# The q, k and v projections of a windowed attention by seven products instead of eight, with a rearranged schedule around them

## The chip, the cores and the metric

The kernel runs on one core of a Trainium2 chip. The metric is the device time of one execution in microseconds. The kernel before took 3387.21 us as the median of three runs (3384.05 to 3391.96).

The engines are named as in the profile: PE is TensorE (matmuls; PEld its weight loads), DVE is VectorE, ACT is ScalarE, POOL is GpSimd, and SP is the queue from which all transfers are issued. Each works through its own instructions in order; they wait for one another by semaphores.

## The reference

An attention layer and a feed-forward layer (FFN), each between two layer norms and with a residual. All values are float32. The batch is 4 x 2048 tokens of 512 features; the FFN has 2048 hidden features and weights of its own for every batch, mixed from eight experts.

```python
x = x + ln(attn(ln(x)))          # ln without scale or offset
x = x + ln(ffn(ln(x)))

def attn(x):                     # 16 heads of 32, windows of 128
    q, k, v = split(x @ w_qkv)
    # a window attends to itself and to the window on either side
    return softmax(q * 32**-0.5 @ k_ctx.T) @ v_ctx

def ffn(x):                      # the batch's weights come from a gate
    h = relu(x @ gate_w1.T + gate_b1)
    g = mean_over_tokens(h @ gate_w2.T + gate_b2)          # [batch, 8]
    mW1, mW2 = W1 + sum_e g[e] * TW1[e], W2 + sum_e g[e] * TW2[e]
    mb1, mb2 = b1 + g @ Tb1, b2 + g @ Tb2
    return gelu(x @ mW1.T + mb1) @ mW2.T + mb2
```

## The kernel before, in words

**Two stages.** The attention comes first, for all four batches; the FFN follows. Tokens are cut into 64 windows of 128 (`W_`) and into 16 blocks of 512 (`K`, four windows each, four blocks a batch). Between the stages, and for the gate, the normalised x lies transposed in DRAM (`xT_d`), the residual in `x1_d`.

**The attention's slots.** A loop over 256 slots (L552) handles window `i // 4` and head group `i % 4` (four heads). Nothing is scheduled by a planner: the order in the source is the order on each engine. In slot i the order is:

1. `first` hooks, then `scores(i + 1)`: four heads' scores on PE (L403) into two PSUM tiles of pool `ps_s`, and two reductions on DVE (L412) for the negative row maxima;
2. `rest` hooks (norms, residuals and their transfers), and from slot 84 on some steps of the mixer (below): 1, 1, 2 and 2 or 3 in the four slots of a window (L563);
3. `turn(i, 0)` and `turn(i, 1)`: transposes of the probabilities on PE (L440), copied from PSUM by ACT (L442);
4. the first half of the slot's `dense` piece, if it has one: four matmul records of a projection (L352) or of the gate (L163) into the single buffer of `ps_m`;
5. two exponentials of slot i + 1 on ACT (L425), `turn(i, 2)`, two more exponentials;
6. the second half of the dense piece, and the reading of its bank (`projected`: q and v by ACT, k by DVE; `gate_sum` by ACT);
7. the first `aux` hook, `values(i)` on PE (L457), the other `aux` hooks.

The hooks of a window `W_` are: in slot 4W_+4 the transposes of its output ("out transposes", L223) and their scaling by DVE with statistics (L230, L88), in 4W_+5 the residual and its store, in 4W_+6 the normalisation `normed`, and in 4W_+7 the transposes of xn2 (L252), copied by ACT and stored to `xT_d`. Each window has tiles `a`, `x1` and `xn2` of its own in two buffers each, and the residual input `xr` in three.

**Projections.** Block K > 0 is projected in the twelve slots from `s0 + 4`, with `s0 = 16K - 20`: four slots for q, four for k, four for v, each one output chunk of 128 features (for v: of 128 tokens) as four matmuls of 512 columns. A float32 matmul is two records in the trace. The four slots ahead of them transpose the block's normalised x (L338, copied by DVE, L339); most of those four have a gate's piece as `dense`. Block 0 is projected ahead of the slots. Slots 12 to 15, 240 to 247 and 252 to 255 have no dense piece.

**The gate.** 15 blocks have their gate in the attention (`gate_at`), the last has all of its gate in the FFN's block 0 (`gate_last`).

**The mixer** (L102) is a generator. A step multiplies one expert's 128 x 1024 piece into an accumulator on DVE (L144), and every ninth step forms sums of quarters (L152 to L155) and later stores them. A step first issues the load for the step three further on, from SP, into four buffers `exps`. There are 4 batches x 2 weights x 8 pieces x 9 = 576 steps; a batch's must be done before its FFN.

**The FFN** already multiplies 2 x 2 blocks by seven products (Strassen-Winograd), with sums of weights from the mixer and sums of x from `right_sums` (L272, `tT`). A block has a first half of four sets (`begin`, `middle`, `end`; matmuls at L606) and a second half of seven products (`second`, `product2`, L699), 6.9 us each. `product2` ends by asking for the weights three products later (`load_second`, L690), which need the buffer that this product reads. Beside them run mixing steps: four in a set, two in each product of the second half; in block 0 none in the sets. At the end of each batch the last block's `end` loads the next batch's first weights (L284).

Of the kernel before, what the change touches and what calls it, by code (L numbers as in the profile page):

```python
# [34 lines left out]
def sandwich(ctx: ExitStack, tc: tile.TileContext, x, w_qkv, gw1, gb1, gw2, gb2, w1, b1, w2, b2, tw1, tb1, tw2, tb2, out):  # L35
# [133 lines left out]

    def gate_end(b, hsum, spare, bank):  # L170
# [47 lines left out]
        b: const.tile([P, KC, NBLK], F32, name=f"hsum_{b}") for b in range(NB)  # L218
# [70 lines left out]
    with ExitStack() as actx:  # L289
        qkvp = actx.enter_context(tc.tile_pool(name="qkvp", bufs=2))  # L290
        work = actx.enter_context(tc.tile_pool(name="work", bufs=2))
        ps_s = actx.enter_context(tc.tile_pool(name="ps_s", bufs=2, space=PSUM))
# [68 lines left out]

        def span_of(W_):
            b, w = divmod(W_, NW)
            lo, hi = max(w - 1, 0), min(w + 1, NW - 1)
            return b * NW + lo, hi - lo + 1

        def open_window(W_):
            win[W_] = {
                "nm": small.tile([P, H], F32, tag="nm", name=f"nm_{W_}"),
                "den": small.tile([P, H], F32, tag="den", name=f"den_{W_}"),  # L370
                "pr": {},
                "prT": {},
            }
            if W_ == NWA - 1:

                win[W_]["oT"] = oT_last
                return
            win[W_] |= {
                "a": work.tile([P, D], F32, tag="a", name=f"a_{W_}"),
                "x1": work.tile([P, D], F32, tag="x1", name=f"x1_{W_}"),  # L380
                "xn2": work.tile([P, D], F32, tag="xn2", name=f"xn2_{W_}"),
                "oT": work.tile([P, KC, P], F32, tag="oT", name=f"oT_{W_}"),
                "xo": work.tile([P, KC, P], F32, tag="xo", name=f"xo_{W_}"),
                "x": load_tile(W_ // WB, W_ % WB, "xr", 3),
            }
# [82 lines left out]
        slots = range(-16, NS + 64)  # L468
        dense = {i: None for i in slots}
# [4 lines left out]
        for K in range(1, NBK):  # L474
            s0 = 4 * (4 * K - 5)
            if K > 1:
                for t in range(WB):
# [5 lines left out]
                    aux[s0 + t].append(lambda K=K, t=t: place_tile(K, t, nc.vector.tensor_copy))  # L483
            for n, i in enumerate((0, 1, 2)):
                for m in range(KC):
                    dense[s0 + 4 + 4 * n + m] = (
                        lambda pm, kcs, K=K, i=i, m=m: project(K, i, m, pm, kcs),
                        lambda pm, K=K, i=i, m=m: projected(K, i, m, pm),
                    )
# [10 lines left out]

        gate_at = {K: 4 * (4 * (K + 3) - 5) for K in range(11)} | {11: 204, 12: 220, 13: 236, 14: 248}
        for K, s0 in gate_at.items():
            first[s0 - 2].append(lambda K=K: load_gate(K))
            for oc in range(KC):
                dense[s0 + oc] = (
                    lambda pm, kcs, K=K, oc=oc: gate_matmuls(pm, gT_of[K], oc, kcs),
                    lambda pm, K=K, oc=oc: gate_sum(pm, K, oc, hsum_of[K // NBLK], spare),
                )
            if K % NBLK == NBLK - 1:
                b = K // NBLK  # L510
                for j, f in enumerate(gate_end(b, hsum_of[b], spare, spare_bank)):
                    late[s0 + KC + j].append(f)

# [5 lines left out]
        for W_ in range(NWA - 1):  # L519
# [3 lines left out]
            aux[4 * W_ + 7].append(lambda W_=W_: via_pt(xn2_transposes, xn2_store, W_, "ptx"))  # L523

        first[240].append(lambda: load_first(0, 0, 0, wp, "w2"))
        first[240].append(lambda: load_block(0))
# [11 lines left out]
        for n, (i, m) in enumerate((i, m) for i in range(3) for m in range(KC)):  # L538
# [3 lines left out]
            projected(0, i, m, pair[:, n % 2, :])  # L542
            if n in (2, 3, 4, 5):
                norm_stats(1, n - 2)
            if n in (5, 6, 7, 8):
                norm_tile(1, n - 5)
            if n in (8, 9, 10, 11):
                place_tile(1, n - 8, nc.vector.tensor_copy)
        scores(0)
        exponentials(0, range(4))  # L550

        for i in range(NS):  # L552
# [4 lines left out]
            if i + 1 < NS:  # L557
                scores(i + 1)

            for f in rest[i]:  # L560
                f()
            if i >= 84:
                for _ in range((1, 1, 2, 2 if W_ % 3 == 2 else 3)[g]):  # L563
# [3 lines left out]
            if dense[i]:  # L567
                pm = ps_m.tile([P, TB], F32, tag="pm", name=f"pm_{i}")
                dense[i][0](pm, range(KC // 2))
            if i + 1 < NS:  # L570
                exponentials(i + 1, (0, 1))
            if nk == 3:
                turn(i, 2)
            if i + 1 < NS:
                exponentials(i + 1, (2, 3))
            if dense[i]:
                dense[i][0](pm, range(KC // 2, KC))
                dense[i][1](pm)
# [7 lines left out]
    with ExitStack() as fctx:  # L586
# [8 lines left out]
        def home(c, i):  # L595
            return (wp, "w2") if c == i == 0 else (wts, f"w1_{c}_{i}")
# [206 lines left out]
        def load_gate_last():  # L803
            gT_last.append(wp.tile([P, KC, TB], F32, tag="w0", name="gT_last"))
            nc.sync.dma_start(gT_last[0], xT_d[NBK - 1])

        def gate_last(oc):
            pm = ps_x.tile([P, 2, Q], F32, tag="xz"[oc % 2], name=f"pmg_last_{oc}").rearrange("p a b -> p (a b)")
            gate_matmuls(pm, gT_last[0], oc)
            gate_sum(pm, NBK - 1, oc, hsum_of[NB - 1], spare)  # L810
# [8 lines left out]
            ("product", 0, 2): [lambda: gate_last(0), lambda: gate_last(1), lambda: gate_last(2), lambda: gate_last(3)],  # L819
# [5 lines left out]
        for c in range(0, HC, 2):  # L825
            for i in range(2):
                if c or i:
# [6 lines left out]
        def step():  # L834
            next(blend, None)

        def steps():
            for _ in range(2):
                next(blend, None)

        def nothing():
            pass

        for K in range(NBK):
# [5 lines left out]
            for c in range(0, HC, 2):  # L850
                n = K * (HC // 2) + c // 2
                S = begin(n)
                middle(n, S, before, step if K else nothing)
# [5 lines left out]
            for j, _ in enumerate(second(K, before, steps, load_x1)):  # L859
# [64 lines left out]
```

## Time and profile before

| what | us |
|---|---|
| median of three runs | 3387.21 |
| the profiled execution | 3387.08 |
| its span, first to last instruction | 3385.3 |
| start of the first FFN matmul (L606) | 1790.34 |
| L352 (projections), both forms, busy on PE | 720.5 |
| L163 (gate, without the last block), busy on PE | 223.9 |
| L440 (turns), busy on PE | 418.4 |
| L144 (mixing), busy on DVE; idle before it for transfers | 693.5; 209.2 |
| ACT prT, pr (L442, L425), busy with the accumulator reads | 1202 |

The page gives, for each engine, the time in which it was busy. PE's busy time says little, since ends of pipelined matmuls are modelled. The chain follows the work that ended last back through whatever released it, piece by piece: a stage whose chain is PE without gaps is set by PE. The timeline lists an engine's instructions with the idle time ahead of them and its releaser. The view of windows gives busy times in stretches, then the granted TensorE clock, the share of the DMA engines and their GB/s.

### The profile page before, as it was taken

Reading aid. Unit: us, or ns where it says so; the run is one execution under the profiler, and the core shown is the slowest. Engines: PE = TensorE matmul, PEld = TensorE weight load, DVE = VectorE, ACT = ScalarE, POOL = GpSimd, SP = SyncE. Lnnn points to the kernel's source line nnn. Section 1 sums busy time; section 2 is a strip of 40 time slices with the busy share of each in tenths; the row PEclk is TensorE's granted clock in tenths of the full one; section 3 lists DMA queues with packets and bytes.
Section 4 is the critical chain, followed back from the end, with each engine's and each line's share of the span. In section 5 each row is a group of like instructions: output and inputs, shape, how many; then the busy total and the mean of one; then the engine's idle time right before and its main releaser. Section 6 shows DMA issues by size and latency. Waiting matters only on the chain.

```text
span 3385.3 us, 55842 instructions
## 1 busy us (share of the span) xinstructions
PE 3333.6 (98%) x21712; PEld 2401.5 (71%) x21712; DVE 2043.7 (60%) x2872; ACT 1484.7 (44%) x3878; POOL 658.0 (19%) x776
## 2 busy tenths in 40 slices
PE   8999999999999999999989999999999999999998
PEld 3555655565555655566558788888888888888887
DVE  2545455688888787887784666677766663222222
ACT  2666666666666666666673111122211122222111
POOL 0100011111111111111002132233223232212222
PEclk9999999999999999999999999999999999999999
DMA  2111111466665666656676788988899883533332
GB/s 82 46 49 42 51 57 51 135 198 203 214 215 184 208 205 197 214 186 203 194 244 228 282 300 292 367 292 299 300 336 356 309 297 140 181 107 112 125 121 78
DMA packets 315194, 651.79 MB, mean 193 GB/s; under 512 B 22953, under 2 KB 88617, under 8 KB 294450
## 3 DMA queue, kind: packets, MB, share of 16 engines
q1 hardware_dynamic: 314930, 648.22, 55.4%
q8 instruction: 171, 2.80, 0.3%
q14 instruction: 93, 0.76, 0.1%
HBM read 538.03 MB, written 110.10 MB: 191 GB/s over the span
## 4 chain that ended last, share of the span: by engine, by line
PE 95%; DMA 2%; DVE 1%; ACT 1%; issue 1%; SPq 0%; DVEq 0%; ACTq 0%
PE pm L352 20%; PE px L606 12%; PE ptp L440 10%; PE px L699 10%; PE pz L699 7%; PE sc L403 7%; PE pm L163 6%; PE pz L606 6%; PE po L457 6%; PE py L699 3%; PE py2b L699 3%; PE py L606 3%; DMA exps<-in_tw 1%; PE ptx L252 1%; PE pto L223 1%; PE pt_a L338 1%
## 5 line engine op out<-in xcount | busy, mean ns | idle before, releaser
L144 DVE SCALAR_TENSOR_TENSOR acc<-exps,g,acc 128x1024 f32<-128x1024 f32 x512 | 693.5, 1355 | 214.2 <-DMA exps<-in_tw 209.2
L442 ACT COPY prT<-ptp 128x512 f32<-128x512 f32 x736 | 407.2, 588 | 525.2 <-PE ptp L440 524.6
L412 DVE TENSOR_REDUCE nm<-sc 128x2 f32<-128x768 f32 (+1 forms) x512 | 448.1, 917 | 257.6 <-PE sc L403 256.7
L425 ACT ACTIVATE pr<-sc,nm 128x384 f32<-128x384 f32 (+1 forms) x1024 | 577.2, 578 | 5.0 <-DVE nm L412 5.0
L440 PEld LDWEIGHTS ptp<-ident,pr 128*128 128x128 f32 x2944 | 332.4, 142 | 223.0 <-issue 204.5
L352 PE MATMUL pm<-xnT,wqkv 128*128 128x512 f32 x1024 | 480.1, 596 | 3.6 <-DVE k L358 1.6
L440 PE MATMUL ptp<-ident,pr 128*128 128x128 f32 x2944 | 418.4, 279 | 5.0 <-ACT prT L442 3.2
L639 ACT COPY cpa<-px 128x512 f32<-128x512 f32 x64 | 37.2, 582 | 793.6 <-PE px L606 793.6
L606 PE MATMUL px<-tT,w 128*128 128x256 f32 x1536 | 358.7, 382 | 10.5 <-DVE cpv L664 10.5
L606 PEld LDWEIGHTS px<-tT,w 128*128 128x128 f32 x1536 | 292.8, 191 | 52.9 <-DVE cpv L664 13.0
L352 PEld LDWEIGHTS pm<-xnT,wqkv 128*128 128x128 f32 x1024 | 177.5, 191 | 144.0 <-issue 136.7
L403 PE MATMUL sc<-k,q 32*128 32x384 f32 (+2 forms) x2816 | 246.2, 422 | 2.9 <-ACT pr L425 2.9
L352 PE MATMUL pm<-wqkv,xnT 128*128 128x512 f32 x512 | 240.4, 593 | 0.5 <-ACT v L360 0.5
L92 POOL TENSOR_SCALAR ve_b<-mv_b 128x1 f32<-128x1 f32 x64 | 14.2, 221 | 1136.8 <-DVE mv_b L90 1084.9
L699 PE MATMUL px<-w2s,u 128*128 128x256 f32 x1024 | 229.5, 380 | 0.7 <-ACT last L257 0.7
L457 PE MATMUL po<-prT,v 128*32 128x128 f32 x5888 | 217.6, 278 | 7.9 <-ACT prT L442 7.7
L457 PEld LDWEIGHTS po<-prT,v 128*32 128x32 f32 x5888 | 144.6, 109 | 112.0 <-issue 93.6
L163 PE MATMUL pm<-gT,gw_sb 128*128 128x512 f32 x480 | 223.9, 593 | 0.0
L425 ACT ACTIVATION_READ_ACCUMULATOR pr<-sc,nm 128x1 f32 x1024 | 217.6, 212 | 0.0
L699 PEld LDWEIGHTS px<-w2s,u 128*128 128x128 f32 x1024 | 195.1, 191 | 27.6 <-ACT last L257 0.9
L676 POOL TENSOR_TENSOR t<-u 128x512 f32<-128x512 f32 x64 | 87.5, 1367 | 465.4 <-ACT u L618 459.3
L403 PEld LDWEIGHTS sc<-k,q 32*128 32x128 f32 x2816 | 119.8, 183 | 58.1 <-issue 28.7
(127 smaller groups left out, 4423.1 us busy)
## 6 DMA issues: line engine op xcount, KB each, us to landing
exps<-in_tw SPq DMA_DIRECT2D x512, 512.0 KB, 5.4
w2s<-m2d SPq DMA_DIRECT2D x112, 1024.0 KB, 5.6
acc<-in_w SPq DMA_DIRECT2D x64, 512.0 KB, 6.0
x<-in_x SPq DMA_DIRECT2D x64, 256.0 KB, 3.1
m1d<-acc SPq DMA_DIRECT2D x64, 256.0 KB, 6.5
m2d<-acc SPq DMA_DIRECT2D x64, 256.0 KB, 6.1
w<-m1d SPq DMA_DIRECT2D x16, 1024.0 KB, 8.5
fxT<-xTd SPq DMA_DIRECT2D x16, 1024.0 KB, 7.4
```

The costliest lines, as they stand in the source:

```text
L144: nc.vector.scalar_tensor_tensor(acc, ets.pop(n), g_all[b][:, e : e + 1], acc, ALU.mult, ALU.add)
L163: nc.tensor.matmul(pm, lhsT=gw1_sb[:, kc, ts(oc, P)], rhs=xT[:, kc, :], start=(kc == 0), stop=(kc == KC - 1))
L352: nc.tensor.matmul(pm, lhsT=l, rhs=r, start=(kc == 0), stop=(kc == KC - 1))
L403: nc.tensor.matmul(scs[r // 2][:, r % 2, col : col + nj * W], lhsT=q[rows, g, ts(W_ % WB, W)], rhs=k_of[kb][rows, g, j0 * W : (j0 + nj) * ...
L412: nc.vector.tensor_reduce(st["nm"][:, h : h + 2], scs[u][:, :, : nk * W], AX.X, ALU.max, negate=True)
L425: nc.scalar.activation(pr[:, : nk * W], scs[r // 2][:, r % 2, : nk * W], AF.Exp, bias=st["nm"][:, h : h + 1], accum_out=st["den"][:, h : h ...
L440: nc.tensor.transpose(pt[:, r, :], st["pr"][g * 4 + r][:, ts(j, W)], ident)
L442: nc.scalar.copy(prT, pt)
L457: nc.tensor.matmul(st["po"][r * E : (r + 1) * E, g, :], lhsT=v_of[kb][:, jj, h * E : (h + 1) * E], rhs=prT[:, r, :], start=(j == 0), stop= ...
L606: nc.tensor.matmul(bank[:, f, :], lhsT=factor[:, f, kc * P : (kc + 1) * P], rhs=right[:, kc, :], start=(start and f == 0 and kc == 0), sto ...
L676: nc.gpsimd.tensor_tensor(t1s[c], b12, S["u"][:, :, :Q], ALU.subtract)
L699: nc.tensor.matmul(bank[:, t, :], lhsT=right(c - c % 2)[:, c % 2, ts(t, P)], rhs=w[:, c, :], start=(start and c == t == 0), stop=True, ski ...
```

## The change

Each of q, k and v of the blocks 1 to 15 is computed by seven products of half-size factors. The operands are cut into quarters of 256 x 256 (features by features for the weights, features by tokens for x); four sums of quarters of either operand are formed by DVE, those of the weights once (`left_factors`, after block 0 has used the weights, one of them in place), those of x for each block (`right_factors`, two operations in each of slots s0+4 and s0+5). A product is four matmuls of 256 columns. Some products add to the bank that an earlier one left in PSUM; ACT copies out four of the seven states of the bank and DVE adds the other three to what has been copied.

A projection still has four slots. In the slot of product 0 it stands alone, in the place of the old dense piece. In the other three an odd product (1, 3, 5) goes between the scores and the turns ("fore"), and the next even one into the old place.

Around it:

- the placing copies of x go from DVE to ACT;
- `a`, `x1` and `xn2` share one tile in two buffers, `xr` has two buffers;
- the xn2 transposes of most windows go one slot later, into the slot of a product 0;
- mixing steps in the attention follow a table of 20 in 16 slots;
- half of the last block's gate goes to slots 254 and 255; the FFN keeps the other half;
- the second tile of the FFN's first weights is loaded early, in slot 240;
- in the FFN the mixing steps are 4 in a set (2 in the last block of a batch that another follows, and in the last two sets of block 0; none in its first two), and 3, 3, 3, 3, 3, 2, 1 in the second half.

```diff
+        def left_factors(i):
+            w = wqkv[i]
+            l11, l12, l21, l22 = (w[:, 2 * j : 2 * j + 2, h * Q : (h + 1) * Q] for h in range(2) for j in range(2))
+            pool, tag = (wp2, f"s{i}") if i else (wp, "w3")
+            s = pool.tile([P, 3, 2, Q], F32, tag=tag, name=f"wsum_{i}")
+            nc.vector.tensor_tensor(s[:, 0], l21, l22, ALU.add)
+            nc.vector.tensor_tensor(l21, l11, l21, ALU.subtract)
+            nc.vector.tensor_tensor(s[:, 1], s[:, 0], l11, ALU.subtract)
+            nc.vector.tensor_tensor(s[:, 2], l12, s[:, 1], ALU.subtract)
...
+        def right_factors(K, part):
...
+            if part == 0:
+                t = work.tile([P, 3, 2, Q], F32, tag="tx", bufs=1, name=f"tx_{K}")
...
+                nc.vector.tensor_tensor(t[:, 0], r12, r11, ALU.subtract)
+                nc.vector.tensor_tensor(t[:, 1], r22, t[:, 0], ALU.subtract)
+            else:
+                t = rights[K]
+                nc.vector.tensor_tensor(r12, r22, r12, ALU.subtract)
+                nc.vector.tensor_tensor(t["T4"], r21, t["T2"], ALU.subtract)
...
+        products = (
+            ("12", "21", True, (0, 0), False),
+            ("11", "11", True, (0, 0), True),
+            ("S2", "T2", False, (0, 1), False),
+            ("S3", "T3", False, (1, 1), False),
+            ("22", "T4", False, (1, 0), False),
+            ("S1", "T1", True, (1, 1), True),
+            ("S4", "22", False, (0, 1), True),
+        )
+        def product(K, i, u, half):
+            l, r, begins, _, _ = products[u]
+            if begins and half == 0:
+                bank[0] = ps_m.tile([P, 2, Q], F32, tag="pm", name=f"pm_{K}_{i}_{u}")
...
+            for kc in range(2):
+                a, b = (left, right) if i < 2 else (right, left)
+                nc.tensor.matmul(
+                    bank[0][:, half, :],
+                    lhsT=a[:, kc, ts(half, P)],
+                    rhs=b[:, kc, :],
+                    start=(begins and half == kc == 0),
...
+        def produced(K, i, u):
...
+            if added and i == 0:
+                nc.vector.scalar_tensor_tensor(to, bank[0], QSCALE, to, ALU.mult, ALU.add)
+            elif added:
+                nc.vector.tensor_tensor(to, bank[0], to, ALU.add)
+            elif i == 0:
+                nc.scalar.mul(to, bank[0], QSCALE)
+            else:
+                nc.scalar.copy(to, bank[0])
...
-                "a": work.tile([P, D], F32, tag="a", name=f"a_{W_}"),
-                "x1": work.tile([P, D], F32, tag="x1", name=f"x1_{W_}"),
-                "xn2": work.tile([P, D], F32, tag="xn2", name=f"xn2_{W_}"),
+                **dict.fromkeys(("a", "x1", "xn2"), work.tile([P, D], F32, tag="x1", name=f"x1_{W_}")),
...
-                    aux[s0 + t].append(lambda K=K, t=t: place_tile(K, t, nc.vector.tensor_copy))
...
+                    aux[s0 + t].append(lambda K=K, t=t: place_tile(K, t, nc.scalar.copy))
+            if K > 1:
+                for part in range(2):
+                    rest[s0 + 4 + part].append(lambda K=K, part=part: right_factors(K, part))
+            for i in range(3):
+                for u in range(7):
+                    (fore if u % 2 else dense)[s0 + 4 + 4 * i + (u + 1) // 2] = (
...
+        rest[252].append(load_gate_half)
+        for n, i in enumerate((254, 255)):
+            ocs = (2 * n, 2 * n + 1)
+            dense[i] = (
...
-            aux[4 * W_ + 7].append(lambda W_=W_: via_pt(xn2_transposes, xn2_store, W_, "ptx"))
+            i = 4 * W_ + 8 if W_ < 58 and W_ % WB != 1 else 4 * W_ + 7
+            aux[i].append(lambda W_=W_: via_pt(xn2_transposes, xn2_store, W_, "ptx"))
...
+            if m == KC - 1:
+                left_factors(i)
...
+        for part in range(2):
+            right_factors(1, part)
...
+        MIXED = (0, 0, 1, 2, 1, 1, 2, 2, 1, 1, 1, 2, 1, 1, 2, 2)
...
+            if fore[i]:
+                fore[i][0](0)
+                fore[i][0](1)
+                if more:
+                    exponentials(i + 1, (0, 1))
+                fore[i][1]()
...
-                for _ in range((1, 1, 2, 2 if W_ % 3 == 2 else 3)[g]):
+                for _ in range(MIXED[i % 16]):
...
-                pm = ps_m.tile([P, TB], F32, tag="pm", name=f"pm_{i}")
-                dense[i][0](pm, range(KC // 2))
-            if i + 1 < NS:
-                exponentials(i + 1, (0, 1))
+                dense[i][0](0)
+            if more:
+                exponentials(i + 1, (2,) if fore[i] else (0, 1))
...
+                if n < 2:
+                    step = mixing(0, 0, 0, 0)
+                elif K == 0 or (k == NBLK - 1 and b + 1 < NB):
+                    step = mixing(0, 1, 0, 1)
+                else:
+                    step = mixing(1, 1, 1, 1)
...
-            for j, _ in enumerate(second(K, before, steps, load_x1)):
+            for j, _ in enumerate(second(K, before, mixing(3, 3, 3, 3, 3, 2, 1), load_x1)):
```

## The prediction

> **What bounds the kernel now.** I read the page first (engine shares and the chain that ended last), then the chain in order of time inside the attention, then the timeline of VectorE (DVE) around a window's first slot, then the busy time by stretches in the feed-forward stage (FFN).
>
> ```profile
> span 3385.3 us, 55842 instructions
> PE 3333.6 (98%) x21712; PEld 2401.5 (71%) x21712; DVE 2043.7 (60%) x2872; ACT 1484.7 (44%) x3878; POOL 658.0 (19%) x776
> PE 95%; DMA 2%; DVE 1%; ACT 1%; issue 1%; SPq 0%; DVEq 0%; ACTq 0%
> ```
>
> TensorE (PE) carries 95% of the chain. One attention slot of the chain shows what is in it:
>
> ```profile
> 1077.60 0.86 PE sc L403 x8
> 1078.46 1.02 PE ptp L440 x8
> 1079.48 1.72 PE pm L352 x4
> 1081.20 0.44 PE ptp L440 x4
> 1081.64 1.72 PE pm L352 x4
> 1083.36 0.79 PE po L457 x24
> 1084.15 0.86 PE sc L403 x8
> ```
>
> The pieces touch: 6.55 us a slot, 3.44 of it the projection (two halves of 1.72). A slot with transposes of xn, out or xn2 has 0.44 more each. So work taken off PE here shortens the kernel until another engine's loop is longer. Slots 240 to 247 have no projection and show that loop:
>
> ```profile
> 1705.16 1.64 PE sc L403 x16
> 1706.80 0.60 PE ptp L440 x4
> 1707.96 0.59 ACT prT L442
> 1708.92 0.78 ACT pr L425 x3
> 1709.69 0.48 ACT prT L442
> 1710.65 1.64 PE sc L403 x16
> ```
>
> A slot then lasts 5.49 us, set by ScalarE's (ACT) copies and exponentials. PE work down to 5.5 us a slot is saved in full, below that nothing is.
>
> **The products.** L352 has 1536 records in 16 blocks, 96 a block, and four of them (512 wide) take 1.72 us: 41.3 us a block. The seven-product form has 3 x 7 products of 8 records 256 wide. In the FFN eight such records take 1.73 us on the same engine (chain: "PE pz L606 x8" 1.73), with their weight loads hidden (191 ns under 216). So 21 x 1.725 = 36.2 us, 5.1 us less a block; blocks 1 to 15 change: **-77 us**. The time leaves the three slots that hold only product 0: 0.86 scores, 1.02 + 0.44 turns, 1.72 product, 0.79 values, 0.44 out transposes and 0.44 xn2 transposes (moved here from a fourth slot, so their sum doesn't change) = 5.71, just above 5.49. ACT has there four exponentials of 0.57 start to start, three copies of 0.55, one bank and the xo copy: 5.1 us. It fits; late queues may cost 0 to 0.3 us in each of 45 slots, I take 0.07: **+3**.
>
> **A new wait, behind product 1.** In nine of sixteen slots an odd product stands between scores and turns, and the even product behind the turns adds to the same bank (ps_m has one buffer). PE comes to it 1.72 + 1.02 = 2.74 us after the scores, and waits until product 1, 3 or 5 has been read. Products 1 and 5 are read by DVE behind both score reductions. When DVE is free the reductions end 1.84 us after the scores (1.82 us for two, started 0.1 after) and the addition, priced as L652, 0.69 us from PSUM, at 2.6: no wait. But behind a product-0 slot DVE isn't free: its out transposes are the last thing on PE before the scores. The timeline has this order in a gate slot:
>
> ```profile
> 1018.21 0.66 PE L223 MATMUL pto<-ident,oT 128*128 128x128 f32 x4
> 1018.91 0.69 DVE L230 TENSOR_TENSOR a<-pto,rden 128x512 f32<-128x512 f32 x1 [0.53 <-PE pto L223]
> 1019.63 0.69 DVE L88 BATCH_NORM_STATS2 st_b<-a 128x6 f32<-128x512 f32 x1
> 1019.68 1.09 PE L440 MATMUL ptp<-ident,pr 128*128 128x128 f32 x8
> 1020.46 1.79 DVE L412 TENSOR_REDUCE nm<-sc 128x2 f32<-128x768 f32 x2
> ```
>
> The reductions end at 1022.25 at the latest, 2.5 us after the scores (the next DVE row starts at 1022.17); addition and signal 0.75 (34.33 to 35.08 at the start of the chain, L358 to PE): 3.24, half a us after 2.74. Behind PE's wait stand a turn, half a product, the values and the next scores. 43 slots have this order (slot 0 has no out transposes, slot 4 has them ahead of the values): **+22 us**, bounds 0 and 43 x 0.9 = 39. Product 3 is read by ACT behind two exponentials, at about 2.75: nothing. An addition with scale for q (a scalar_tensor_tensor with PSUM) has no row; by L144 (1355 ns for 1024) it is 0.68.
>
> **The rest of DVE and ACT in the attention.** Per 16 slots DVE gains 9 additions and 4 right sums (0.6 start to start) and loses 4 k copies, 4 placing copies and about 6.7 mixing steps of 1.3: 3 us added, 8.7 less. ACT gains 8 evacuations of 0.55, 4.4 us; it is 66 to 69% busy. Hidden while slots stay above 5.5. In slots 12 to 15, which have no projection, the placing copies are on ACT's loop: **+1.5**. xn2 now overwrites x1, so its normalisation waits for x1's store: that lands in 2.2 us (row "x1d<-x") and was issued most of a slot (6.5 us) earlier: 0. The third buffer of xr and the moved xn2 stores have a slot of slack each: 0; 2 us each if not.
>
> **The start.** The left factors of v (three of four operations after PE has read the weights, 0.6 each) and the four right sums of block 1 stand on DVE before the first scores are reduced, where the chain has DVE xnT then nm: 7 x 0.6 = 4.2, less about 0.5 under PE's last transposes. PE's idle time grows to some 6 us, after which the clock may be halved for one 3.41 us window (the trace's clock record has such windows after the stalls near 2150 and 2550): **+5** (3.5 to 6).
>
> **End of the attention.** Half of the last block's gate (13.7 us, L163 in the FFN) goes to slots 254 and 255, which have no projection: -6.9 there, and the two slots, 4.3 to 5 us now, get 3.44 of PE work each, about +2.2. The granted clock is half from 1793.2 to 1803.5, after those thin slots, costing 5.1 us; I count half of it as saved. The gate's load waits for window 61's store and holds SP's queue for some us: three mixing loads are ahead of need. **-7** (-2 to -10). Slot 243 runs one mixing step less in DVE's 10 us backlog: **-1.5**.
>
> **Mixing.** There are 576 steps. In the attention there were 287, now 217; so the FFN has 359 instead of 289. At the batch changes (blocks 3 and 7) eight weight loads collide with 30 steps: DMA share 0.95, 359 GB/s, and the blocks take 103.9 and 104.6 us against 96.7. With half the steps in their first halves, 4.2 MB less, this should go: **-15**.
> The price is in the second halves: three steps beside each of products 0 to 4 instead of two.
>
> ```profile
> 2349.80:2356.70 6.90, 6.90 (x34) 6.07 (x33) 4.21 (x3) 0.99 (x3) 1.60 (x1) 1.00 0.20 69
> 2377.40:2384.30 6.90, 6.90 (x34) 6.07 (x33) 3.17 (x3) 0.00 (x0) 0.00 (x0) 1.00 1.04 372
> 2384.30:2391.20 6.90, 6.90 (x34) 6.07 (x33) 3.08 (x3) 0.00 (x0) 0.00 (x0) 1.00 1.03 411
> ```
>
> The last column is GB/s; all six products to 2391.2 moved 69, 270, 340, 262, 372, 411. The first moved little because the mixing loads stand in SP's queue behind the w2s load, which waits for PE to finish the product. Today DVE's addition behind product 5 comes 0 to 6.3 us after the product (2396.28 against 2391.24 here), on average 3. PE notices when the first tT sum isn't ready 8.6 us after product 5, that is at a lag of 6.8. Five more steps by then are 5 x 0.68 MB (0.52 for the expert, 0.16 for its share of base and stores) = 3.4 MB. At 400 GB/s products 1 to 5 have 2.4 MB unused, so 1 MB or 2.4 us is added to the lag: 5.4 on average, over 6.8 only in the worse blocks, about 1 us a block in blocks 0 to 10: **+11**. The Trainium skill, "DMA: Bandwidth & Descriptors", Specifications, gives about 358 GB/s of HBM per core and so speaks against this change: then 0.9 MB are unused, the lag grows by 6.9 to 9.9 and the stall is 3.1 x 11 = 34 us. The row of 411 is nearer, though it holds for 7 us only; I take 11 and keep 34 for the range.
>
> **Sum.** -77 + 3 + 22 + 1.5 + 5 - 7 - 1.5 - 15 + 11 = -58. The profiled execution took 3387.1 us (1.8 outside the span), the median is 3387.2: 3329.
>
> **Rivals.**
> (a) Clean: DVE is in time behind product 1 and the lag stays under 6.8: -58 - 22 - 11 = -91, 3296. For it: steps leave DVE in these slots. Against: the chain behind the out transposes is serial. Chance 0.17.
> (b) DVE or ACT is late in all nine odd slots, 135 x 0.5 = 67 instead of 22: 3374. For it: the margin of products 3 and 5 is 0.1 us. Against: no out transposes stand before them, and steps are fewer. 0.10.
> (c) Slower: not bandwidth but SP's order and four exps buffers set the pace in the second halves. The six products averaged 287 GB/s; if that stays, 11.9 + 3.4 MB take 53.3 instead of 41.4 us, the lag is 3 + 11.9, PE stalls 8.1 us in 11 blocks, +89 instead of +11: 3407. It decides from 6.3 us a block, an average below 297 GB/s. Against it: 340 to 411 wherever loads were queued. 0.09.
> (d) The forecast: 0.64, between 3305 and 3357 by its bounds.
> That the products don't take less PE time would need 256-wide records to be dearer here than in the FFN; both have the same shape.
>
> **Range and chances.** 3298 to 3370 leaves out (c), most of (b) and the lower half of (a). A measurement tells 0.2% (7 us) from no change. Faster 0.89, within 0.2% 0.03, slower 0.08.
>
> **What would show it.** The chain of one block: 21 pieces of 1.72 for pm, 16 slots in about 107 us instead of 110; a piece of about 0.5 us, released by DVE, ahead of product 2 and not ahead of products 4 and 6; ACT in no product-0 slot's chain. FFN blocks 3 and 7 near 97 us; idle before L606 (tT) released by DVE, 0 to 4 us a block. Wrong if the attention (the first L606, 1790.3) ends less than 30 us earlier, or if blocks 1 to 10 pass 100 us.

## The result, and the profile after

The changed kernel takes 3393.72 us (median of 12 runs, 3390.37 to 3400.09) against 3386.11 us for the kernel before beside it (12 runs). The ratio is 1.0023, with an interval of 1.0014 to 1.0032: 0.2% slower, where 58 us less were forecast.

The page after, in the lines that answer to those of before (span; busy time of the engines; share of each in the chain that ended last):

```profile
span 3393.3 us, 58421 instructions
...
PE 3308.6 (98%) x22824; PEld 2615.8 (77%) x22824; DVE 2104.8 (62%) x2963; ACT 1532.1 (45%) x4002; POOL 642.7 (19%) x776
...
PE 81%; DVE 8%; DMA 6%; ACT 3%; issue 1%; SPq 0%; DVEq 0%; ACTq 0%
```

PE is busy 25 us less in 8 us more. Its share of the chain has fallen from 95% to 81%, and VectorE (DVE), transfers and ScalarE (ACT) stand in it with 17%: PE waits.

By stage, the trace gives: first FFN matmul at 1789.65 us (before 1790.27 in the same view), so the attention gained 0.6 us where the forecast's steps up to there add up to some 45. FFN block 0 became 7.7 us shorter (half of the last gate left it), blocks 1 to 11 together 16.5 us longer.

**The attention, slot by slot.** Durations from the start of one slot's scores to the next, medians by position in the period of 16, slots 96 to 143. The last two columns belong to experiments below. Positions 3, 7 and 15 held the xn2 transposes before (0.44 us at 3 and 7) and don't now; they stand at 4, 8 and 0.

| position (products) | before | after | read late | out transposes first |
|---|---|---|---|---|
| 0, 4, 8 (0) | 6.98 to 7.01 | 5.87 to 5.90 | 5.87 to 5.90 | 5.87 to 5.90 |
| 1, 5, 9 (1, 2) | 6.55 to 6.58 | 7.26 | 6.63 to 6.69 | 6.86 to 6.90 |
| 2, 6, 10 (3, 4) | 6.55 to 6.58 | 6.93 to 6.97 | 7.13 to 7.15 | 6.93 to 6.97 |
| 3, 7 (5, 6) | 6.99 | 6.86 to 6.87 | 6.62 | 6.86 to 6.87 |
| 11 (5, 6), xn2 transposes as before | 7.01 | 7.33 | 7.08 | 7.32 |
| slots 96 to 112 together | 110.54 | 109.93 | 107.98 | 108.79 |

The slots of product 0 give 3.3 us a period, where the forecast's 5.71 us a slot would have given 3.8. The slots with two products give it back: 2.1 us at positions 1, 5 and 9, 1.15 us at 2, 6 and 10. Positions 3, 7 and 11 are 0.3 us each above what they were without the transposes that left 3 and 7. The chain of the changed kernel through positions 1, 2 and 3 shows how (start and duration in us, engine, tile):

```profile
720.34 0.60 PE pto L248 x4
720.96 0.70 DVE x L255
...
722.60 0.85 DVE nm L512
...
724.22 0.69 DVE q L456
724.96 1.13 PE pm L438 x4
...
731.39 0.50 ACT q L460
731.93 1.13 PE pm L438 x4
...
736.01 1.92 PE pm L438 x8
737.93 0.87 PE ptp L540 x8
738.81 1.12 PE pm L438 x4
```

In each slot the first half of the even product (the last PE line of each group) takes 1.12 or 1.13 us where four records 256 wide need 0.86. Ahead of it stands the reading of the bank: at position 1 by DVE, late behind the out transposes' scaling (the forecast wait); at position 2 by ACT; at position 3 the chain doesn't even leave PE, and the half still takes 1.12.

**The FFN.** From one block's last product to the next one's, blocks 1 to 8 took 98.9, 96.7, 103.9, 97.0, 96.7, 96.8, 104.6 and 96.7 us before; after, they take 102.8, 97.6, 102.4, 101.6, 102.0, 97.6, 99.7 and 98.9. Two stretches of a second half in the changed kernel (its products 0 and 1 after the first quarter of product 0; the columns are those of the windows before):

```profile
2353.60:2360.50 6.90, 6.90 (x33) 6.08 (x33) 5.69 (x4) 1.17 (x3) 1.61 (x1) 1.00 0.23 75
2360.50:2367.40 6.90, 6.90 (x33) 6.07 (x33) 3.25 (x5) 0.00 (x0) 3.79 (x3) 1.00 0.83 294
```

The transfers move 75 GB/s at first, then 294; in the five products after that, 376 to 407. The chain of this stretch then has

```profile
2374.96 9.09 DMA exps<-in_tw
...
2388.05 0.70 DVE y L861
2388.79 7.17 PE px L842 x32
```

A mixing load lands after 9.09 us, DVE's queue is late by that, and PE waits for a sum of y behind it. In the list of waits for the whole FFN these are "PE pz L749 <- DVE tT L301: 12.1, 7, 2.6" and "PE px L842 <- DVE y L861: 7.7, 7, 1.7" (total, times, longest): 19.8 us of PE. The kernel before has neither of them, and one of 10.5 us in their stead ("PE px L606 <- DVE cpv L664: 10.5, 3, 4.9").

### The profile page after: what moved, and what is told of

Same layout as the page of the kernel before. It is cut to its first block, busy times and chain, and to the rows that moved or that the text cites. A ratio compares the mean times of both kernels' runs of the same rounds, so it can differ in the third digit from the quotient of the medians.

```text
span 3393.3 us, 58421 instructions
## 1 busy us (share of the span) xinstructions
PE 3308.6 (98%) x22824; PEld 2615.8 (77%) x22824; DVE 2104.8 (62%) x2963; ACT 1532.1 (45%) x4002; POOL 642.7 (19%) x776
## 4 chain that ended last, share of the span: by engine, by line
PE 81%; DVE 8%; DMA 6%; ACT 3%; issue 1%; SPq 0%; DVEq 0%; ACTq 0%
PE pm L438 13%; PE px L749 12%; PE ptp L540 8%; PE px L842 7%; PE pz L749 6%; PE pmg L163 6%; PE po L557 6%; PE sc L503 6%; DMA exps<-in_tw 5%; PE pz L842 5%; PE py L749 3%; PE py L842 3%; DVE nm L512 3%; ACT pr L525 2%; PE py2b L842 1%
## 5 line engine op out<-in xcount | busy, mean ns | idle before, releaser
L540 PEld LDWEIGHTS ptp<-ident,pr 128*128 128x128 f32 x2944 | 344.0, 142 | 102.2 <-issue 61.3
L540 PE MATMUL ptp<-ident,pr 128*128 128x128 f32 x2944 | 410.4, 277 | 2.9 <-ACT prT L542 2.9
L749 PE MATMUL px<-tT,w 128*128 128x256 f32 x1536 | 355.4, 379 | 0.8 <-DVE cpv L807 0.8
L749 PEld LDWEIGHTS px<-tT,w 128*128 128x128 f32 x1536 | 291.6, 190 | 41.3 <-DVE cpv L807 1.8
L842 PE MATMUL px<-w2s,u 128*128 128x256 f32 x1024 | 229.9, 380 | 8.4 <-DVE y L861 7.7
L163 PE MATMUL pmg<-gT,gw_sb 128*128 128x512 f32 x480 | 223.9, 593 | 0.0
L842 PEld LDWEIGHTS px<-w2s,u 128*128 128x128 f32 x1024 | 193.7, 190 | 38.0 <-DVE y L861 11.2
L438 PE MATMUL pm<-xnT,wqkv 128*128 128x256 f32 x720 | 182.4, 391 | 0.0
L438 PEld LDWEIGHTS pm<-xnT,wqkv 128*128 128x128 f32 x720 | 128.6, 191 | 39.3 <-issue 13.5
L749 PE MATMUL pz<-tT,w 128*128 128x256 f32 x512 | 126.6, 392 | 12.1 <-DVE tT L301 12.1
```

Of the source, the lines that this page charges most:

```text
L163: nc.tensor.matmul(pm, lhsT=gw1_sb[:, kc, ts(oc, P)], rhs=xT[:, kc, :], start=(kc == 0), stop=(kc == KC - 1))
L438: nc.tensor.matmul(bank[0][:, half, :], lhsT=a[:, kc, ts(half, P)], rhs=b[:, kc, :], start=(begins and half == kc == 0), stop=True, skip_g ...
L540: nc.tensor.transpose(pt[:, r, :], st["pr"][g * 4 + r][:, ts(j, W)], ident)
L749: nc.tensor.matmul(bank[:, f, :], lhsT=factor[:, f, kc * P : (kc + 1) * P], rhs=right[:, kc, :], start=(start and f == 0 and kc == 0), sto ...
L842: nc.tensor.matmul(bank[:, t, :], lhsT=right(c - c % 2)[:, c % 2, ts(t, P)], rhs=w[:, c, :], start=(start and c == t == 0), stop=True, ski ...
```

## The experiments

Times are medians; each ratio is against the kernel before in runs on the same chip. "After" is the changed kernel.

**The two halves of the change, apart.** First the kernel before with only the new mixing schedule, then after with the old one.

```diff
# mixing alone, on the kernel before; products alone: the reverse, on the changed kernel
-                for _ in range((1, 1, 2, 2 if W_ % 3 == 2 else 3)[g]):
+                for _ in range(MIXED[i % 16]):
...
-            for j, _ in enumerate(second(K, before, steps, load_x1)):
+            for j, _ in enumerate(second(K, before, mixing(3, 3, 3, 3, 3, 2, 1), load_x1)):
```

> The kernel before with the mixing schedule of the changed kernel alone (20 steps in 16 slots of the attention, the new counts in the FFN). The theory: the second halves with three steps a product outrun the transfers and PE waits for the first tT sum and for the additions, while the attention gains nothing, since PE sets its slots: the attention ends at 1790 as before, the FFN's blocks 1 to 10 take 97 to 102 us, in all 10 to 17 us more than before, about 3400. The rival, as the prediction had it: the relief at the batch changes (15 us) outweighs the price (11): 3383. If the FFN blocks stay at 96.7 the loss in the changed FFN comes from something else.

> The changed kernel with the mixing schedule of before, in the attention and in the FFN. The theory: the FFN gets back about 16 us (blocks 3 and 7 at 104, the others at 96.7 to 97), and the attention keeps its waits for the reading of the bank; with more steps on DVE its slots are as long or a little longer (0 to 10 us): 3377 to 3387. The rival: the mixing table is what keeps DVE in time, so that the attention grows by over 20 us and the sum is above 3400.

Mixing alone: 3403.18 us, ratio 1.0043 (1.0032 to 1.0055). Products alone: 3383.90, ratio 0.9987 (0.998 to 0.9994). With mixing alone the period stays at 110.54 us and blocks 1 to 8 take 104.2, 97.6, 100.7, 102.6, 101.7, 98.3, 99.2 and 99.1. Blocks 1 to 11 together take 18.2 us more than before (16.5 in after), so the FFN's loss is that of the schedule. (Its attention ends 5.4 us earlier, and block 0, which now has mixing steps, takes 4.4 us more.) With the products alone blocks 3 and 7 take 103.1 and 102.7 and the others 96.7 to 98.9, and block 0 is 7.7 us shorter by the half gate: that is the small gain. Positions 1, 5 and 9 take 7.26 us with either mixing schedule, so it isn't mixing steps on DVE that make the odd slots wait.

**The read of the bank.** In after, the odd product's bank is read only when the even product has been added to it. The state with the odd product alone is then never copied out, so q, k and v are not those of the reference; the number of operations is the same.

```diff
                     exponentials(i + 1, (0, 1))
-                fore[i][1]()
...
                 dense[i][0](1)
+                if fore[i]:
+                    fore[i][1]()
                 dense[i][1]()
```

> The changed kernel, but an odd product's bank is read only after the even product has been added to it, so that PE has nothing to wait for between the two. The values of q, k and v are then not the reference's; every instruction is still there. The theory: the waits for the reading cost 4.3 us of 16 slots, so slots with an odd product go from 7.3 and 6.9 to 6.55 to 6.7 us, 16 slots from 110 to about 106, the attention ends 55 to 65 us earlier: about 3332. The rival: products 256 wide are dearer here whatever they wait for (weights not loaded ahead, turns delayed): slots stay within 0.1 us of 7.3 and 6.9, above 3385.

One run: 3367.21 us, 26.5 below after. The attention ends 34.7 us earlier, where 55 to 65 were expected. The chain at the start of a slot of position 2, then in one of position 3:

```profile
711.65 0.61 ACT q L460
...
712.30 1.99 PE pm L438 x8
...
720.91 0.87 PE ptp L540 x8
721.78 0.86 PE pm L438 x4
```

Where the wait is gone, the first half takes 0.86 (last line) and the slot 6.62, against 6.55 before and 6.87 after: two products in this form cost some 0.06 us more than the old piece, and the wait 0.25 (in the chain 1.12 us for the half against 0.86, that is 0.26). Positions 2, 6 and 10 rise to 7.13 instead, since both reads now stand behind the even product and the next odd product waits for them (first two lines). The wait moved to the next user of the single bank. That is what the expectation missed.

What these 0.26 us are made of is in the timeline of PE and of its weight loads (PEld), at the start of the same half at position 1. First with the read late:

```profile
707.72 0.73 PEld L438 LDWEIGHTS pm<-tx,wsum 128*128 128x128 f32 x4
707.83 1.03 PE L438 MATMUL pm<-tx,wsum 128*128 128x256 f32 x4
```

Then with the read in its place (the kernel with the out transposes first, below):

```profile
719.03 0.73 PEld L438 LDWEIGHTS pm<-tx,wsum 128*128 128x128 f32 x4 [0.22 <-DVE q L456]
719.03 1.13 PE L438 MATMUL pm<-tx,wsum 128*128 128x256 f32 x4
```

Without a wait the first weights are loaded 0.11 us ahead of the product, under the turns. With one, the load itself waits for DVE, and some 0.1 is added (1.13 against 1.03). The other 0.15 is the wait: the turns began at 718.01 and need 0.87.

DVE's rows at this place, with the start of the turns, show what the read waits for:

```profile
716.28 1.82 DVE L512 TENSOR_REDUCE nm<-sc 128x2 f32<-128x768 f32 x2 [0.63 <-PE sc L503]
718.01 1.04 PE L540 MATMUL ptp<-ident,pr 128*128 128x128 f32 x8
718.28 0.69 DVE L456 SCALAR_TENSOR_TENSOR q<-pm,q 128x512 f32<-128x512 f32 x1 [0.18 <-PE pm L438]
```

The reductions end at 718.10. The addition still waits 0.18 us, for product 1 itself. It starts 0.27 us behind the start of the turns, takes 0.69, and the half starts 0.06 behind its end: 1.02 us on the way to DVE and back, against 0.87 of turns in between.

**Out transposes first.** They go ahead of the values where an odd product follows in the next slot, so that DVE scales them under the values; xn2's go behind.

```diff
-            aux[4 * W_ + 4].append(lambda W_=W_: via_pt(out_transposes, out_scaled, W_, "pto"))
+            at = aux[4 * W_ + 4]
+            at.insert(0 if fore[4 * W_ + 5] else len(at), lambda W_=W_: via_pt(out_transposes, out_scaled, W_, "pto"))
```

> The changed kernel with the out transposes ahead of the values in the slots of a product 0, and the xn2 transposes behind them. The theory: DVE starts the scaling and the statistics 1.2 us earlier and is free when the scores end, so the slot behind falls from 7.26 to the 6.9 of its neighbours: 0.35 x 43 = 15 us, 3378. The rival: the wait there is set by ACT or by PE's own order, and nothing changes (3393).

3379.47 us, ratio 0.9976 (0.9965 to 0.9986); the first FFN matmul comes 18 us earlier than in after. Positions 1, 5 and 9 fall by 0.36 to 0.40, to the level of the other odd slots. So DVE's work behind the out transposes is worth 17 us of the loss; some 0.26 remains in all nine slots (by the timeline 0.15 of wait at positions 1, 3, 5, 7, 9 and 11, 0.22 at 2, 6 and 10 where ACT reads, and everywhere the late weights).

**Reading in halves, and the mixing evened.** Three kernels on top of the last: mixing steps 20 beside a block's sets and two beside every product; the bank read in two halves; both.

```diff
# mixing evened
+                else:
+                    step = mixing(1, 1, 1, 2)
...
-            for j, _ in enumerate(second(K, before, mixing(3, 3, 3, 3, 3, 2, 1), load_x1)):
+            for j, _ in enumerate(second(K, before, mixing(2, 2, 2, 2, 2, 2, 2), load_x1)):
# read in halves
-                fore[i][1]()
+                fore[i][1](0)
+                fore[i][1](1)
```

> The kernel with the out transposes moved ahead of the values, and in the FFN the mixing steps spread otherwise: 20 beside the four sets of a block and two beside every product, instead of 16 and 3, 3, 3, 3, 3, 2, 1. Theory (five steps too many beside products 1 to 5, whose loads can't start in products 0 and 1 because they stand in SP's queue behind a w2s load that waits for PE): blocks 1, 2, 4 to 6 and 8 to 10 fall from 98 to 103 us to 96.7 to 98, about 2.5 us less in eight to eleven blocks, so 20 to 27 us less than the 3379.5 measured without the spreading: 3352 to 3360. Rival (the same number of bytes in a block is too much wherever it stands): the steps moved into the sets stop PE there, blocks stay at 99 to 103, 3375 to 3385.

> The kernel with the out transposes moved ahead of the values, and the odd product's bank read in two halves of 256 columns, one for each half of the even product that follows. Theory (the even product waits for the end of the read, and what it loses is the tail of the read's own time): the wait ends about 0.3 us earlier in each of nine odd slots of sixteen, slots of 6.9 us fall to about 6.65, 15 x 9 x 0.25 = 34 us less, 3346[...]. Rival (the wait is the start of the read, late on ACT and DVE because of what stands ahead of it, and the matmuls behind a wait load their weights late in any case): the slots stay within 0.1 us of 6.9, 3366 to 3380.

> The two edits together: mixing evened and the odd product's bank read in halves. They act in different stages, so theory: the sum of their gains, about 3326 us (3379.5 - 20 - 34). If reading in halves gains nothing, about 3358; if the spreading gains nothing, 3346; if neither does, 3380.

Evened: 3365.73 us, ratio 0.9932 (0.9912 to 0.9951), 14 us below "out transposes first" where 20 to 27 were expected; blocks 1 to 10 take between 96.7 and 102.1. In halves: 3389.29, 1.0003 (0.9993 to 1.0013). Both: 3373.33, 0.9959 (0.9943 to 0.9975). Reading in halves lost, alone and on top of evened: all nine odd slots became some 0.06 us longer (135 x 0.06 = 8). The timeline of that kernel at position 1:

```profile
718.71 0.76 DVE L459 SCALAR_TENSOR_TENSOR q<-pm,q 128x256 f32<-128x256 f32 x2 [0.19 <-PE pm L438]
...
719.52 1.13 PE L438 MATMUL pm<-tx,wsum 128*128 128x256 f32 x4
```

PE starts 0.05 us after the end of the second read (719.47), not of the first: in this kernel it waits for both halves. Whether that lies in the program's semaphores or in the chip is not shown. So the run doesn't tell what an earlier first half would give. It does show that the end of the read sets all nine slots: a read that is longer by 0.07 makes them longer by 0.06.

**The order of the w2s loads.** On top of "out transposes first", the load for the product three further on is issued behind this product's mixing loads; then the same edit alone on the kernel before.

```diff
# in product2
-            load_second(7 * K + j + 3)
# in second, in each of the seven places
             steps()
+            load_second(7 * K + j + 3)
```

> The kernel with the out transposes moved ahead of the values, and in the FFN's second halves each w2s load issued behind the product's mixing loads on SP's queue instead of ahead of them; the steps are the same 3, 3, 3, 3, 3, 2, 1. Theory (it is SP's order that leaves the transfers idle in products 0 and 1, 30 to 139 GB/s, so that what follows is saturated at 400): the mixing loads start early, the second halves lose their stalls, blocks fall from 98 to 103 us towards 97, 15 to 25 us less: 3355 to 3365. Rival (bandwidth: three steps and a w2s load in 6.9 us ask for more than the 400 GB/s measured): the first products gain what the last ones lose, blocks stay at 99 to 102, 3372 to 3380; the w2s loads, then behind others, may come too late and make PE wait: more than 3380.

> The kernel before, with nothing changed but the place of the w2s load in the FFN's second halves: behind the product's mixing loads on SP's queue instead of ahead of them. Theory (SP's order delays the mixing loads whatever the number of steps): of the 18 us by which the blocks of before exceed 96.7 most goes in blocks 1 to 7, but blocks 3 and 7 (103.9 and 104.6), which have eight weight loads and 30 steps each, stay at 100 or more by their bytes: 8 to 12 us less, 3376 to 3379. Rival (the order matters only with three steps beside a product): within 3 us of before.

With the change: 3349.24 us, ratio 0.9882 (0.9865 to 0.9899), the fastest kernel here, 30 us below the same kernel without the edit. On the kernel before: 3375.37, 0.997 (0.9958 to 0.9981). The same first two stretches of the same block, in the kernel with the edit:

```profile
2318.30:2325.20 6.90, 6.90 (x34) 6.07 (x33) 5.63 (x4) 1.10 (x3) 1.61 (x1) 1.00 0.95 304
2325.20:2332.10 6.90, 6.90 (x34) 6.07 (x33) 6.62 (x7) 0.00 (x0) 4.49 (x3) 1.00 0.95 309
```

304 GB/s instead of 75 at the start. What held the transfers is in SP's waits of the changed kernel from 2340 to 2402 us (total, times, longest; L833 is the w2s load):

```profile
SPq L833 <- PE px L842: 10.8, 2, 8.0
```

SP stood 8.0 us at a load whose buffer PE was still reading, and every mixing load behind it stood too. With the edit, blocks 1 to 8 take 98.9, 97.5, 96.7, 98.1, 96.7, 96.7, 97.4 and 98.6. In the kernel before, blocks 3 and 7 fall from 103.9 and 104.6 to 98.6 and 98.9, with all of their eight weight loads and 30 steps in place.

**The odd product elsewhere.** On top of the 3349.24: first between the two halves of the scores; then ahead of the scores with the reads ahead of reductions and exponentials, and the last two exponentials behind the read of the even product; then the same with these exponentials back in place where no odd product follows.

```diff
# inside the scores
+                if u == 0:
+                    between()
# before the scores
+            if fore[i]:
+                fore[i][0](0)
+                fore[i][0](1)
+                fore[i][1]()
             if more:
                 scores(i + 1)
# last exponentials
+            read_first = bool(fore[i] and fore[i + 1])
-            if more and not fore[i]:
+            if more and not read_first:
                 exponentials(i + 1, (2, 3))
```

> The kernel with the out transposes ahead of the values and the w2s loads behind the mixing loads (3349.2), and the odd product put between the two halves of the scores instead of behind them, so that half of the scores and the two turns (1.46 us instead of 1.02 on PE) stand between it and the even product on the same bank, and DVE reads the bank between its two reductions. Theory (the 0.26 us that an odd slot still loses between the turns and the end of the even product's first half, 0.15 of it in the wait for the bank's read and 0.11 because a waiting product's first weights aren't loaded under the turns, both end when the read is done before the turns are): the nine odd slots fall from 6.86 to 6.97 us to 6.60 to 6.70, 15 x 9 x 0.26 = 35 us less, 3314. Rival 1 (the pieces are dearer by their borders, not by the wait: a product behind the scores loads its first weights late wherever it stands, and one more border is added): slots at 6.9 to 7.0, 3345 to 3365. Rival 2 (the wait moves: the second half of the scores reaches the exponentials 1.7 us later, or the odd product now waits for the read of the bank behind the even one): some slots fall and others rise, 3330 to 3350.

> The kernel with the out transposes ahead of the values and the w2s loads behind the mixing loads (3349.2), and in the nine odd slots of sixteen the odd product put ahead of the scores, its bank read ahead of the two reductions (DVE) and of the exponentials (ACT), and the last two exponentials behind the reading of the even product's bank. The scores stay together, and they and two turns (1.9 us) stand between the odd product and the even one. Theory (0.15 us of wait and 0.11 us of late weights between the turns and the even product go, a border of 0.1 to 0.2 us ahead of the odd product stays, now behind the values instead of behind the scores): odd slots fall from 6.86 to 6.97 us to 6.65 to 6.75, 15 x 9 x 0.2 = 27 us less, 3322. Rival (the odd product now stands 0.8 us behind the even one of the slot before and waits for the reading of that bank by ACT or DVE: the wait is moved, not removed; or the exponentials, which start 1.9 us later, hold up the turns): slots at 6.9 to 7.3, 3350 to 3400.

> The kernel with the odd product ahead of the scores (3358.9), but where the next slot has no odd product the last two exponentials stand ahead of the reading of the even product's bank again, as they do in the change. Theory (in 45 slots of product 0 the scores waited 0.62 us for these two exponentials, 1.48 us in the chain instead of 0.86, because they were behind the bank's read by DVE or ACT; this alone hid the gain of the odd slots, which fell from 6.9 to 6.77): the period of sixteen slots falls from 109.4 to 107.5 to 108.1 us, 15 x 1.5 = 22 us less, 3337, below the 3349.2 of the odd product behind the scores. Rival (the scores of product-0 slots then wait for something else, or product 1 ahead of the scores waits for product 0's bank): no more than 8 us less, 3350 or over.

Inside: 3441.58 us, ratio 1.0162 (1.0147 to 1.0177). Before the scores: 3358.86, 0.9918 (0.9897 to 0.9939). Last exponentials: 3360.17, 0.9918 (0.9904 to 0.9931).

Inside the scores, every odd slot became 0.7 us longer, for a reason that was in neither theory. The chain:

```profile
702.17 0.84 PE sc L505 x4
703.01 1.92 PE pm L438 x8
704.94 0.84 PE sc L505 x4
```

Two heads' scores take 0.84 us, and four heads' took 0.86: each head uses 32 of the 128 rows, and by these times four run side by side. Cutting them in two costs a whole score time. The product behind the turns does take 0.86 there: the wait is gone, as the theory has it.

Ahead of the scores the pure odd slots fall to 6.77 to 6.80 us, 0.1 us below the 6.86 to 6.97 of the order with the product behind the scores: the half takes 0.86, but the turns now stand behind the scores and take 1.02 instead of 0.87. And at positions 4 and 8 a slot of product 0 together with the odd product that follows takes 8.50 us instead of 5.87 + 1.92: its scores take 1.48 us in the chain. First such a slot, then a pure odd one behind the values:

```profile
739.65 1.48 PE sc L503 x8
741.13 1.02 PE ptp L540 x8
...
752.99 1.93 PE pm L438 x8
754.91 0.86 PE sc L503 x8
```

The last experiment took away what I held for the cause, and nothing changed. Its timeline, at the same place:

```profile
742.24 0.30 PEld L503 LDWEIGHTS sc<-k,q 32*128 32x128 f32 x4 [0.34 <-ACT pr L525]
```

The scores still wait for an exponential. What I take from it, without a run that shows it: exponentials that start 1.9 us later end later whatever stands at their end, and the scores need their two PSUM tiles. The theory on their order fell; of the three places, the one behind the scores is the best. The kernel of 3349.24 us beats before and after; it together with the evened mixing wasn't tried.

## Why the prediction was wrong

- **The products (-77).** PE's work was costed nearly right: the slots of product 0 came out at 5.87 us for 5.71, and the form with two products costs 0.06 us a slot that the sum did not have.
- **"A new wait, behind product 1" (+22): the step that failed.** The half microsecond that it charged to 43 slots is there: at position 1 of the changed kernel the turns start at 723.57 and need 0.87, and the half starts at 724.96, 0.52 us later. But it took products 3 and 5 for "no wait" and "nothing", with a margin of 0.1 us. Shown in its place: in all nine odd slots of a period the even product loses about 0.26 us, 0.15 (0.22 behind ACT) at the bank's read and 0.11 because a weight load isn't pulled ahead of a wait. The step dated DVE's read from the end of the reductions and put its end at 2.6 us after the scores. The read cannot start before its product has ended, and in the rows above it is that end which releases it: the half starts 2.85 us after the scores (716.18 to 719.03), where the turns would have let PE start at 2.70. 135 slots x 0.26 are 35 us, and 17 more for DVE's work behind the out transposes: 52 where the sum had 22. The Trainium skill, "TensorE: Matmul & The Clock Gate", Part 2, says that PE pulls weight loads ahead of matmuls that are running; the two timelines above agree, and the second shows a load that was not pulled ahead of a wait.
- Rival (b), late in all nine odd slots at 0.5 us (67 us), was nearest for the attention. Slots 16 to 240 hold fourteen of the fifteen blocks. There the trace gives -4.0 us, where the forecast's steps, taken for fourteen blocks, add up to -48. The runs account for it: -71.4 for the products, 16.0 for DVE's work behind the out transposes, 126 x 0.26 = 32.8, 126 x 0.06 = 7.6 for the form, 42 x 0.16 = 6.7 for product 0 (3 were forecast), and 3 x 2.2 = 6.6 at the batch changes (113.5 to 115.1 us where other periods fell by 0.6), together -1.7. Of the rest 1.9 us lie in the kernel before, whose first mixing loads hold up one of these periods (115.4 us, the two others like it 113.5). The term of the batch changes is from the trace only: there the gate's end stands on DVE ahead of the bank's reading. No run took it apart.
- **The start (+5), the end of the attention (-7).** +3.9 in slot 0; -7.7 in block 0 of the FFN and +2.5 behind slot 254. The sums are near enough, but the clock was misplaced by 11.3 us: the windows before show a granted clock of 0.50 from 1781.9 to 1792.1 us and 1.00 from 1793.2 to 1803.5, so the half clock lay on the last slots and only 2 us of the FFN. Afterwards it is 1.00 from 1780 to 1815 us, and 0.57 instead of 1.00 from 66 to 70 us, in slot 0. How much of the two sums is the clock was not taken apart.
- **"Mixing" (-15 and +11): wrong in the cause, and 20 us off.** Blocks 3 and 7 gained 6.5, not 15, and the other blocks lost 23, not 11. The step read 0.95 of the DMA share as bytes in the way. The order alone, on the kernel before, took these blocks to 98.6 and 98.9 with the same bytes. The thing was in sight: the prediction says itself that the loads "stand in SP's queue behind the w2s load", and then counts GB/s.
- **Rival (c)** named the right mechanism, SP's order, but with a price of 89 us in place of the 11; it was 23, since the later products do reach 376 to 407 GB/s. These rates, over 35 us, also speak against the estimate of 34 us that the prediction worked out from 358 GB/s.

## What to carry to other kernels

Splitting one matmul piece into two on the same PSUM bank makes a round trip to another engine part of the loop. Date the read from the end of the product that it reads, not only from what stands ahead of it on the reading engine. Count the reading engine's whole time plus the hand-over (0.27 us before the read and 0.06 behind it here) against what PE has to do in between, in every place, and doubt margins of 0.1 us.

Look at a queue's own waits before counting its bytes: one load that waits for its buffer at the head of SP's in-order queue cost 30 us here, with the same bytes to move.

Before putting another matmul between small ones, see whether they already run side by side.

## What the runs showed of the hardware

- Four heads' scores on 32 rows each take 0.86 us, two heads' 0.84. Eight product records behind scores or values take 1.92 us, behind turns twice 0.86; eight turn records take 1.02 behind scores and 0.87 behind a product. The Trainium skill, "TensorEngine Tiling (Array Packing)", Key Properties, says that tiles run independently, and also that a change of the tiling mode drains the array. The scores agree with the first, and these borders with the second; no run here takes a border apart.
- The first weights of a matmul that waited for a read of its bank were loaded with it and not 0.11 us ahead: the half then took 1.13 us instead of 1.03.
- One core's transfers held 376 to 407 GB/s over five products, 35 us.
